# Gate and up of a transformer block: the issuing queue of the moving tiles, the places of the act sums, and the pools of the down projection

## The chip, the cores and the metric

One core of one Trainium2 chip runs the whole program. The metric is the device time of one execution in microseconds (us). The kernel before took 3004.6 us (median of three runs, 3001.72 to 3014.55).

## The reference: what is computed

The reference is one transformer block on two sequences of 1024 positions and 1024 features, in float32:

```
h = layernorm(x) * (1 + ca) + sa
x = x + ga * attention(h)
h = layernorm(x) * (1 + cb) + sb
gate = einsum(h, Wg) * ag
up   = einsum(h, Wu) * au
x = x + gb * (einsum(silu(gate) * up, Wd) * ad)
```

The attention has 32 heads of 32, a causal mask with linear position biases, and layer norms on queries and keys. Wg and Wu have 2752 rows of 1024, and Wd 1024 rows of 2752. The shifts, scales and gates (sa, ca, ga and so on) come from a product of a small vector with a modulation matrix.

## The kernel before

**Order of the work.** The program runs the modulation and the QKV projections, then the attention with dense work in between, the output projection and what is left of the rows, then gate and up (from about 1560 us to 2497 us), then down (to the end). The change lies in the last two.

**Tiling.** Gate and up use Strassen's scheme in Winograd's form on two levels. 2560 of the 2752 inner columns are cut into five slices of 512 (the index s); the other 192 are handled apart. For each slice, the outer level has seven stages (STAGES, in the order A11, A12, S1, S2, S4, S3, A22) and the inner level has seven products in each stage (CHAIN). A product is a gate matmul pair and an up matmul pair, each of four matmuls of 128x512 in the trace, on the same moving tile. The four PSUM banks of a stage are gx, ux, gy and uy: inner products that end in column x or y of the result. One product is 3.43 us of TensorE, one stage 24.0, one slice 168.2.

**Moving tiles.** `moving` (line 1648) allocates a tile bt of 512 KB in a pool of six buffers and loads it from DRAM, where the operands of both levels have been written earlier (bop_T and bop_B). The first six go through ScalarE's queue, all others through SyncE's (SP). A load waits until the product that used the buffer six loads ago has been done.

**Reads of PSUM.** `merge` (line 1566) takes each inner product out of its bank: a copy on ScalarE where there is nothing to add (1576, 1584), else an addition on VectorE (1578, 1582, 1586) into the outer results X, C, Z and T. The results of gate have one buffer each; uX has two. Within a stage several products go on accumulating in one bank, and the next matmuls into it wait for the read between; the stages take two sets of four banks in turn.

**GpSimd.** `gate_sums` (1623 to 1630) builds the outer sums of the weights of a slice, eight operations; `gate_inner` (1632) builds the inner sums (sig and siu) of each stage, eight operations in two buffers. In the first twenty stages a slice of down's weights is prepared as well: `down_load` loads wdr (1179), `down_weights` does four subtractions on GpSimd (1185 to 1188) and stores the results (wdop, 1190), with one buffer of wdr.

**Due times.** `after(n, go)` puts an operation into a list that is due when n more products have been issued; `run_due` issues those that are due after each product, and ties each to stand behind the last read of PSUM on VectorE (`behind`). So the operations beside the products are placed by product counts, while the order in each engine is what these counts give.

**Results of a slice.** `final(x_, m, q, n)` takes an outer result to its end: two Silus on ScalarE (1703) at count n, two products gate x up on VectorE (1707) at count n + 1, and a store. The act sums S1 to S4 that down's own outer level needs (two halves l, four sums each, 1783) are due 3 to 6 products after the end of the slice; SP stores each (1784). The next slice's first write into gX has to wait for the products that read the old gX.

**Down.** `stage_weights` (1837) loads the quarters B11, B12, B21, B22 of the prepared down weights for an outer stage and builds T1 to T4 on VectorE (1846 and following); act tiles (aq) are loaded at 1856, their inner sums (dsi) are built at 1862 to 1865, and the matmuls are at 1876. The pools of this part lie over space that gate and up give back.

Of the kernel before, what the change touches and what calls it, by code (L numbers as in the profile page):

```python
# [12 lines left out]
FP = mybir.dt.float32  # L13
# [5 lines left out]
P = 128  # L19
# [461 lines left out]
def kernel(  # L481
# [19 lines left out]
    nc = tc.nc  # L501
# [6 lines left out]
    HALF = D // 2  # L508
# [1079 lines left out]
    with ExitStack() as ff:  # L1588
# [9 lines left out]
        with ExitStack() as gu:  # L1598
# [45 lines left out]
                    )  # L1644
                return ins

            def moving(s, n_, i, eng=nc.sync):
                qb_ = CHAIN[i][2]
                bt = bsp.tile([P, NJ, 2, P], FP, tag="bt", name=f"bt_{s}_{n_}_{i}")
                eng.dma_start(bt, bop_dram[STAGES[n_][1]][:, INNER.index(qb_)])  # L1650
                return bt


            W = gate_weights(0, nc.scalar)
            ins = gate_inner(W, 0, 0)
            bts = [moving(0, 0, i, nc.scalar) for i in range(6)]
            rest_st.close()
            ffp.append(ff.enter_context(tc.tile_pool(name="ff_a", bufs=4, space=PSUM)))
            ptp, rxp, rcp = open_("fpart"), open_("resx"), open_("resc")
# [22 lines left out]
            for s in range(NSB):  # L1682
                if s:
                    W = gate_weights(s)
                gate_sums(W)
                res = {}

                def result(mat, x_):
                    if (mat, x_) not in res:
                        res[mat, x_] = (rxp if x_ == "X" else rcp if x_ == "C" else rzp).tile(  # L1690
                            [P, 2, 2, 512], FP, tag=f"{mat}{x_}", name=f"{mat}{x_}_{s}",
                            bufs=2 if (mat, x_) == ("u", "X") else None,
                        )
                    return res[mat, x_]

                def final(x_, m, q, n, res=res, s=s):


                    g, u = res["g", x_], res["u", x_]

                    def silu(l):
                        ib = 4 * s + 2 * m + l
                        nc.scalar.activation(g[:, l], g[:, l], AF.Silu, scale=vt[:, R_AG + ib : R_AG + ib + 1])

                    def product(l):
                        ib = 4 * s + 2 * m + l
                        r = nc.vector.scalar_tensor_tensor(
                            u[:, l], u[:, l], vt[:, R_AU + ib : R_AU + ib + 1], g[:, l], ALU.mult, ALU.mult
                        )
                        if l and q != "A21":  # L1710
                            nc.sync.dma_start(act_dram[q][:, s], u)
                        return r

                    for l in range(2):
                        after(n, lambda l=l: silu(l))
                    for l in range(2):
                        after(n + 1, lambda l=l: product(l))

                for n_, (oa, ob, frm, to) in enumerate(STAGES):
                    if (s, n_) == (0, 2):  # L1720
                        pair_st.close()
                        rzp, asp = open_("resz"), open_("asum")
                    if (s, n_) != (0, 0):
                        ins = gate_inner(W, s, n_)
                        bts = []
                    bank = {
                        (mat, c_): ffbank(f"{mat}{c_}_{s}_{n_}")
                        for mat in ("g", "u")
                        for c_ in ("x", "y")
                    }  # L1730
                    part = {"g": {}, "u": {}}
                    tiles = {
                        mat: (None if frm is None else result(mat, frm), result(mat, to)) for mat in ("g", "u")
                    }
                    i = next(slices, None)
                    if i is not None:
                        wd_ = down_load(i, dwp)
                        after(5, lambda i=i, wd_=wd_: down_weights(i, wd_))
                    for e, (c_, qa, qb_, q) in enumerate(CHAIN):
                        bt = bts[e] if e < len(bts) else moving(s, n_, e)  # L1740
                        for mat in ("g", "u"):
                            ps = bank[mat, c_]
                            for c2 in range(2):
                                nc.tensor.matmul(  # L1744
                                    ps.rearrange("p (j t) -> p j t", j=NJ), ins[mat][qa][:, c2, :], bt[:, :, c2, :],
                                    start=(q in ("P1", "P2", "P5") and c2 == 0), stop=(c2 == 1),
                                    skip_group_check=True,
                                )
                            f_, t_ = tiles[mat]
                            merge(  # L1750
                                q, ps, lambda m, n: t_[:, m, n, :],
                                None if f_ is None else (lambda m, n: f_[:, m, n, :]),
                                part[mat], ptp, f"{mat}_{s}_{n_}",
                            )
                        count[0] += 1
                        run_due()
                    if oa == "A12":
                        final("C", 0, "A11", 1)
                    elif oa == "S2":
                        for m, n in QUADS:  # L1760
                            for mat in ("g", "u"):
                                nc.gpsimd.tensor_add(
                                    result(mat, "T")[:, m, n], res[mat, "X"][:, m, n], res[mat, "Z"][:, m, n]
                                )
                    elif oa == "S3":
                        for m, n in QUADS:
                            for mat in ("g", "u"):
                                z = res[mat, "Z"][:, m, n]
                                nc.gpsimd.tensor_add(z, res[mat, "X"][:, m, n], z)
                        final("Z", 1, "A22", 5)  # L1770
                    elif oa == "S4":
                        final("T", 0, "A21", 1)
                    elif oa == "A22":
                        final("X", 1, "A12", 1)

                a11, a12, a21, a22 = (res["u", x_] for x_ in ("C", "X", "T", "Z"))
                for l in range(2):
                    sm_ = {
                        q: asp.tile([P, 2, 512], FP, tag=q, name=f"as{q}_{s}_{l}") for q in ("S1", "S2", "S4")
                    }  # L1780

                    def go(q, op, dst, x_, y_, s=s, l=l):
                        r = op(dst, x_, y_)
                        nc.sync.dma_start(act_dram[q][:, s, l], dst)
                        return r

                    for e, (q, op, dst, x_, y_) in enumerate((
                        ("S1", nc.vector.tensor_add, sm_["S1"], a21[:, l], a22[:, l]),
                        ("S2", nc.vector.tensor_sub, sm_["S2"], sm_["S1"], a11[:, l]),
                        ("S3", nc.vector.tensor_sub, a21[:, l], a11[:, l], a21[:, l]),  # L1790
                        ("S4", nc.vector.tensor_sub, sm_["S4"], a12[:, l], sm_["S2"]),
                    )):
                        after(3 + (4 * l + e) // 2, lambda go=go, r=(q, op, dst, x_, y_): go(*r))
            run_due(True)


        with tc.tile_pool(name="wdq", bufs=1) as wdp, tc.tile_pool(name="aq", bufs=3) as aqp, tc.tile_pool(
            name="wdt", bufs=1
        ) as wtp, tc.tile_pool(
            name="ais", bufs=3  # L1800
        ) as aip, tc.tile_pool(name="dres", bufs=1) as drp, tc.tile_pool(
            name="dpart", bufs=2
        ) as dpp, tc.tile_pool(name="fin", bufs=3) as fnp, tc.tile_pool(
            name="drest", bufs=1
        ) as dlp:
            gb = []
            ra = [dlp.tile([P, B, NJ, 2, P], FP, name=f"ra{r}") for r in range(2)]
            rw = [dlp.tile([P, D], FP, name=f"rw{r}") for r in range(2)]
# [25 lines left out]
                    nc.gpsimd.tensor_add(x1, x1, c_[:, th])  # L1834
                    nc.sync.dma_start(out[b, ts(2 * i + th, P), ts(n, HALF)], x1)

            def stage_weights(ob, eng):
                wt = {
                    q: (wtp if q[0] == "T" or q == "B12" else wdp).tile(
                        [P, NSB, 256], FP, tag=q, name=f"wd_{ob}_{q}", bufs=2 if q == "B22" else 1  # L1840
                    )
                    for q in ("B11", "B12", "B21", "B22", "T1", "T2", "T3", "T4")
                }
# [8 lines left out]
            def products(n_, i, wt):  # L1852
# [15 lines left out]
                    c_: ffbank(f"d{c_}_{n_}_{i}")[:, 0:256] for c_ in ("x", "y")  # L1868
                }
                if (to, i) not in res:  # L1870
                    res[to, i] = drp.tile([P, 2, HALF], FP, tag=f"{'T' if to == 'C' else to}{i}", name=f"d{to}_{i}")
                f_, t_ = None if frm is None else res[frm, i], res[to, i]
                part = {}
                for c_, qa, qb_, q in CHAIN:
# [37 lines left out]

            running = []
            for n_ in range(len(STAGES)):
                wt = stage_weights(STAGES[n_][1], nc.sync if n_ else nc.scalar)
                for i in range(NJ):
                    if n_ == 0 and i == 2:
                        rest_loads()
# [59 lines left out]
```

## Time and profile before

| Quantity | Value |
|---|---|
| Median of three runs | 3004.6 us (3001.72 to 3014.55) |
| Profiled execution, its own time | 3009.32 us |
| Span of its profile | 3007.6 us |
| Granted TensorE clock, mean | 0.962 |
| TensorE (PE) busy | 2743.3 us, 91% |
| VectorE (DVE) busy | 1506.9 us, 50% |
| GpSimd (POOL) busy | 1289.1 us, 43% |
| ScalarE (ACT) busy | 686.6 us, 23% |
| Transfers | 579.12 MB, mean 193 GB/s |

The profile is of one execution, 4.7 us above the median of the runs. "Busy" is the time in which an engine has an instruction under way; an idle engine that others don't wait for costs nothing. Lines of a timeline give the start (us from the span's start), the duration, the engine, the line of the kernel, the operation, the tiles written and read, how many instructions are joined (x), and in brackets the idle time before it and what ended it. SPq and ACTq are the queues of SyncE and ScalarE in which transfers are issued. Lines of a view of waits give the engine and line that waited, what it waited for, and the total, the number and the longest of these waits in us.

By stretches, the profile shows for gate and up:

| Stretch, us | TensorE busy | ScalarE busy | GpSimd busy | Share of DMA |
|---|---|---|---|---|
| 1603 to 1705 | 101.10 of 102 | 9.31 | 59.54 | 0.81 |
| 1705 to 1780 | 64.78 of 75 | 8.09 | 43.36 | 0.79 |
| 1780 to 1843 | 41.06 of 63 | 4.06 | 41.08 | 0.72 |
| 1843 to 1963 | 120.00 of 120 | 11.01 | 57.87 | 0.66 |
| 1963 to 2497 | 515.12 of 534 | 55.37 | 261.13 | 0.65 |

The first slice and the first part of the second lie before 1843, the slices 2, 3 and 4 after 1963.

### The profile page before, as it was taken

The page shows a single profiled execution, that of the slowest core. Times are in us where ns is not written, and L with a number is a line of the kernel's source. Part 1 is how long each engine was busy: PE and PEld are TensorE (multiplying, and loading weights), DVE is VectorE, ACT ScalarE, POOL GpSimd, SP SyncE. Part 2 cuts the span into 40 slices and gives each one's busy share as a digit, 9 for nine tenths or more (in the row PEclk, how much of TensorE's full clock was granted, in tenths as well). Part 3 has the DMA queues.
Part 4 walks back from the last instruction along what each step waited for, and adds up shares of the span by engine and source line. Part 5 has one row for each costly group of instructions (what it writes and reads, how often), then busy time and mean ns, then how long its engine had stood idle before and what let it go on. Part 6 is the DMA issues. An engine that isn't in the chain of part 4 may idle for free.

```text
span 3007.6 us, 29795 instructions
## 1 busy us (share of the span) xinstructions
PE 2743.3 (91%) x10271; PEld 1341.0 (45%) x10271; DVE 1506.9 (50%) x2285; ACT 686.6 (23%) x1523; POOL 1289.1 (43%) x1150
## 2 busy tenths in 40 slices
PE   7999999999998879787996978999999998999998
PEld 2444333333332222223662433434444346888776
DVE  5666424566443456555553334464634545444453
ACT  1322144444434455552110011010101100000000
POOL 3211033334354555654465564564735441222343
PEclk9999999999999899998997999999999998999999
DMA  9877753534525545335777777675666659554542
GB/s 338 295 257 292 265 210 113 188 130 157 190 88 194 140 150 165 103 109 151 219 244 245 242 248 255 183 260 166 223 218 193 218 164 274 147 158 139 150 143 78
DMA packets 377571, 579.12 MB, mean 193 GB/s; under 512 B 21590, under 2 KB 278712, under 8 KB 366276
## 3 DMA queue, kind: packets, MB, share of 16 engines
q1 hardware_dynamic: 359768, 554.54, 56.5%
q10 hardware_dynamic: 17644, 22.59, 2.5%
q8 instruction: 84, 1.38, 0.2%
q14 instruction: 75, 0.61, 0.1%
HBM read 411.89 MB, written 165.17 MB: 192 GB/s over the span
## 4 chain that ended last, share of the span: by engine, by line
PE 39%; DMA 7%; POOL 6%; issue 5%; DVE 3%; ACT 1%; SPq 1%; POOLq 0%; ACTq 0%; DVEq 0%
PE gx L1744 7%; PE ux L1744 6%; PE dx L1876 6%; PE dy L1876 5%; PE gy L1744 5%; PE uy L1744 4%; PE bank L745 2%; PE sc L745 1%; DMA wdr<-in_L_ffn_Wd_dram 1%; ACT p L1053 1%; DMA wdop_T<-wdr 1%; PE rest L745 1%; DMA bt<-bop_B 1%; PE av L745 1%; POOL p L1085 1%
## 5 line engine op out<-in xcount | busy, mean ns | idle before, releaser
L1053 ACT ACTIVATE p<-sc,kw 128x128 f32<-128x128 f32 (+3 forms) x1024 | 422.1, 514 | 335.2 <-PE sc L745 324.0
L745 PE MATMUL bank<-wT,a 128*128 128x512 f32 x768 | 361.9, 614 | 14.1 <-DVE wT L814 7.2
L1085 POOL TENSOR_TENSOR p<-p,p 128x1024 f32<-128x1024 f32 (+3 forms) x128 | 264.2, 2064 | 252.3 <-PE av L745 223.4
L1085 DVE TENSOR_TENSOR p<-p,p 128x1024 f32<-128x1024 f32 (+3 forms) x192 | 247.5, 1301 | 119.4 <-POOL p L1057 70.5
L745 PE MATMUL bank<-wB,a 128*128 128x512 f32 x576 | 263.8, 602 | 2.1 <-DVE raw L947 1.3
L745 PE MATMUL sc<-cq,ck 32*128 32x512 f32 (+3 forms) x1536 | 195.0, 549 | 68.8 <-ACT p L1053 68.6
L1057 POOL TENSOR_SCALAR_AFFINE_SELECT p<-p 128x256 f32<-128x256 f32 x256 | 137.5, 548 | 229.5 <-ACT p L1053 226.3
L745 PEld LDWEIGHTS bank<-wT,a 128*128 128x128 f32 x768 | 142.5, 195 | 201.2 <-issue 181.0
L745 PE MATMUL av<-p,cv 128*32 128x512 f32 (+3 forms) x1536 | 170.6, 512 | 4.7 <-POOL p L1057 4.7
L745 PEld LDWEIGHTS bank<-wB,a 128*128 128x128 f32 x576 | 104.4, 190 | 146.9 <-issue 127.6
L1744 PE MATMUL gy<-bt,sig 128*128 128x512 f32 x280 | 139.4, 622 | 27.4 <-DVE gX L1582 13.2
L745 PEld LDWEIGHTS sc<-cq,ck 32*128 32x128 f32 x1536 | 65.6, 188 | 199.8 <-ACT p L1053 118.1
L1744 PE MATMUL gx<-bt,sig 128*128 128x512 f32 x280 | 134.9, 605 | 4.4 <-DMA bt<-bop_T 2.3
L1744 PE MATMUL uy<-bt,siu 128*128 128x512 f32 x280 | 132.2, 594 | 0.6 <-DMA bt<-bop_B 0.6
L1744 PE MATMUL ux<-bt,siu 128*128 128x512 f32 x280 | 131.6, 592 | 0.0
L949 DVE TENSOR_TENSOR raw<-P,bank 128x512 f32<-128x512 f32 x48 | 32.9, 685 | 158.0 <-PE bank L745 142.7
L1744 PEld LDWEIGHTS gy<-bt,sig 128*128 128x128 f32 x280 | 54.6, 198 | 98.7 <-issue 80.4
L1744 PEld LDWEIGHTS gx<-bt,sig 128*128 128x128 f32 x280 | 54.2, 196 | 76.9 <-issue 74.6
L745 PEld LDWEIGHTS av<-p,cv 128*32 128x32 f32 x1536 | 33.4, 110 | 121.3 <-issue 87.6
L1744 PE MATMUL gx<-bt,wgA 128*128 128x512 f32 x120 | 58.4, 610 | 28.5 <-DVE gX L1582 27.9
L1744 PEld LDWEIGHTS uy<-bt,siu 128*128 128x128 f32 x280 | 53.5, 191 | 68.7 <-issue 68.0
L1744 PEld LDWEIGHTS ux<-bt,siu 128*128 128x128 f32 x280 | 53.2, 190 | 67.0 <-issue 66.3
(416 smaller groups left out, 4583.5 us busy)
## 6 DMA issues: line engine op xcount, KB each, us to landing
bt<-bop_T SPq DMA_DIRECT2D x140, 512.0 KB
bt<-bop_B SPq DMA_DIRECT2D x99, 512.0 KB
a<-hop SPq DMA_DIRECT2D x20, 1792.0 KB
wm<-in_L_wmod_dram SPq DMA_DIRECT2D x48, 512.0 KB
wB<-in_L_attn_Wqkv_dram SPq DMA_DIRECT2D x21, 1024.0 KB
aq_S<-act_S SPq DMA_DIRECT2D x16, 1280.0 KB
qk<-qs SPq DMA_DIRECT2D x16, 1024.0 KB
act_S<-asS SPq DMA_DIRECT2D x30, 512.0 KB
```

The costliest lines, as they stand in the source:

```text
L745: return in_order(nc.tensor.matmul(*args, **kw_))
L949: nc.vector.tensor_add(dst, part_t[MATE[q]], bank)
L1053: nc.scalar.activation(p[:, g, lo:hi], sp[:, g, lo:hi], AF.Exp, bias=kw[:, d, h_ : h_ + 1])
L1057: nc.gpsimd.affine_select(out=p[:, :, 0:P], in_=p[:, :, 0:P], pattern=[[0, 2], [1, P]], compare_op=ALU.is_ge, fill=0.0, base=0, channel_mu ...
L1085: adders[b](half, jb).tensor_add(dst, dst, ps[half][:, :, 0:n])
L1744: nc.tensor.matmul(ps.rearrange("p (j t) -> p j t", j=NJ), ins[mat][qa][:, c2, :], bt[:, :, c2, :], start=(q in ("P1", "P2", "P5") and c2 ...
L1876: nc.tensor.matmul(bank[c_], ins[qa][:, s, :], wt[qb_][:, s, :], start=(q in ("P1", "P2", "P5") and s == 0), stop=(s == NSB - 1), skip_gro ...
```

## The change

1. All moving tiles are issued from ScalarE's queue.
2. In `final`, the second product gate x up is due one count after the first instead of together with it.
3. The act sums are put into the list at the end of stage S3 and not at the end of the slice. Z's Silus are due at count z = 4 (2 in the last slice) instead of 5. S1, S2 and S3 of the two halves are due at z + 2 to z + 4, which is around the end of the slice, and S4 at 11 and 12, counted from the end of S3. S2 has two buffers.
4. The pools of down are opened in another order and packed otherwise: the second buffer of B22 becomes a pool of its own for odd stages (`late`), the X results have a pool of their own, and the inner sums of act have two buffers instead of three. Which of the tiles lie over space that is free early changes with this.

```diff
-            def moving(s, n_, i, eng=nc.sync):
+            def moving(s, n_, i):
                 qb_ = CHAIN[i][2]
                 bt = bsp.tile([P, NJ, 2, P], FP, tag="bt", name=f"bt_{s}_{n_}_{i}")
-                eng.dma_start(bt, bop_dram[STAGES[n_][1]][:, INNER.index(qb_)])
+                nc.scalar.dma_start(bt, bop_dram[STAGES[n_][1]][:, INNER.index(qb_)])
                 return bt
...
                     for l in range(2):
-                        after(n + 1, lambda l=l: product(l))
+                        after(n + 1 + l, lambda l=l: product(l))
+
+                def act_sums(z, res=res, s=s):
+                    a11, a12, a21, a22 = (res["u", x_] for x_ in ("C", "X", "T", "Z"))
+
+                    def go(q, op, dst, x_, y_, l):
+                        r = op(dst, x_, y_)
+                        nc.sync.dma_start(act_dram[q][:, s, l], dst)
+                        return r
+
+                    for l in range(2):
+                        s1, s2, s4 = (
+                            asp.tile([P, 2, 512], FP, tag=q, name=f"as{q}_{s}_{l}", bufs=2 if q == "S2" else 1)
+                            for q in ("S1", "S2", "S4")
+                        )
+                        for e, r in enumerate((
+                            ("S1", nc.vector.tensor_add, s1, a21[:, l], a22[:, l]),
+                            ("S2", nc.vector.tensor_sub, s2, s1, a11[:, l]),
+                            ("S3", nc.vector.tensor_sub, a21[:, l], a11[:, l], a21[:, l]),
+                            ("S4", nc.vector.tensor_sub, s4, a12[:, l], s2),
+                        )):
+                            n = 7 + 4 + l if e == 3 else z + 2 + (3 * l + e) // 2
+                            after(n, lambda r=r, l=l: go(*r, l))
...
-                        final("Z", 1, "A22", 5)
+
+                        z = 4 if s < NSB - 1 else 2
+                        final("Z", 1, "A22", z)
+                        act_sums(z)
...
-                        after(3 + (4 * l + e) // 2, lambda go=go, r=(q, op, dst, x_, y_): go(*r))
...
+        with ExitStack() as dn:
+            wdp, aqp, wtp, aip, dpp, dxp, late, drp, fnp, dlp = (
+                dn.enter_context(tc.tile_pool(name=n, bufs=k))
+                for n, k in (
+                    ("wdq", 1), ("aq", 3), ("wdt", 1), ("ais", 2), ("dpart", 2), ("dresx", 1),
+                    ("wdl", 1), ("dres", 1), ("fin", 3), ("drest", 1),
+                )
+            )
...
-            def stage_weights(ob, eng):
+            def stage_weights(ob, odd, eng):
                 wt = {
-                    q: (wtp if q[0] == "T" or q == "B12" else wdp).tile(
-                        [P, NSB, 256], FP, tag=q, name=f"wd_{ob}_{q}", bufs=2 if q == "B22" else 1
+                    q: (wtp if q[0] == "T" or q == "B12" else late if q == "B22" and odd else wdp).tile(
+                        [P, NSB, 256], FP, tag=q, name=f"wd_{ob}_{q}"
                     )
...
-                wt = stage_weights(STAGES[n_][1], nc.sync if n_ else nc.scalar)
+                wt = stage_weights(STAGES[n_][1], n_ % 2, nc.sync if n_ else nc.scalar)
```

More of the change, by code (lines that the diff above doesn't have):

```diff
@@ L1655 @@
             ins = gate_inner(W, 0, 0)
-            bts = [moving(0, 0, i, nc.scalar) for i in range(6)]
+            bts = [moving(0, 0, i) for i in range(6)]
             rest_st.close()
@@ L1774 @@
                         final("X", 1, "A12", 1)
[L1776 to L1792, printed above, removed]
-                        after(3 + (4 * l + e) // 2, lambda go=go, r=(q, op, dst, x_, y_): go(*r))
-            run_due(True)
[L1797 to L1805, printed above, removed]
+            run_due(True)
+        with ExitStack() as dn:
[6 more added lines that the diff above has]
+            )
             gb = []
@@ L1870, in products @@
                 if (to, i) not in res:
-                    res[to, i] = drp.tile([P, 2, HALF], FP, tag=f"{'T' if to == 'C' else to}{i}", name=f"d{to}_{i}")
+                    res[to, i] = (dxp if to == "X" else drp).tile([P, 2, HALF], FP, tag=f"{'T' if to == 'C' else to}{i}", name=f"d{to}_{i}")
                 f_, t_ = None if frm is None else res[frm, i], res[to, i]
```

## Prediction

> **What bounds the kernel now.** I first read the page: TensorE is busy 91% of the span and the granted clock is 0.96, so only idle TensorE can be won. The change touches nothing before the gate/up part, so I then asked the waits of TensorE from 1590 us (end of the rest rows) to 2530 us (first products of down); columns are total us, times, longest:
>
> ```profile
> PE gx L1744 <- DVE gX L1582: 27.9, 1, 27.9
> PE gy L1744 <- DMA bt<-bop_B: 26.4, 6, 11.5
> PE gy L1744 <- DVE gX L1582: 13.2, 3, 4.5
> PE dx L1876 <- DVE dsi_A L1863: 11.6, 1, 11.6
> PE gx L1744 <- DMA bt<-bop_T: 4.9, 5, 1.8
> ...
> PE dx L1876 <- DMA aq_A<-act_A: 2.6, 1, 2.6
> ```
>
> Four places hold nearly all of it: one wait at the start (27.9, ended 1603.9), the moving tiles (26.4 + 4.9 and smaller ones, some 37 in all, mostly before 1825), three boundaries between slices (13.2), and the start of down (11.6 + 2.6).
>
> *Moving tiles.* The timeline of SP's queue where the two longest waits lie (the ones that end at 1796.65 and 1819.86):
>
> ```profile
> 1792.97 1.34 SPq L1784 DMA_DIRECT2D act_S<-asS  x2
> 1795.34 0.32 SPq L1784 DMA_DIRECT2D act_S<-uT  x1
> 1796.58 13.60 SPq L1784 DMA_DIRECT2D act_S<-asS  x3
> 1813.14 0.32 SPq L1784 DMA_DIRECT2D act_S<-uT  x1
> 1814.80 0.32 SPq L1784 DMA_DIRECT2D act_S<-asS  x1
> 1815.21 3.36 SPq L1650 DMA_DIRECT2D bt<-bop_B  x6
> ```
>
> No moving tile is issued for 22 us, because stores of the act sums wait for VectorE in the same queue. Six come out at once when they are through.
>
> *A boundary.* TensorE, VectorE and GpSimd where slice 2 begins (1963.32):
>
> ```profile
> 1973.62 1.88 PE L1744 MATMUL uy<-bt,siu 128*128 128x512 f32 x4
> 1979.93 3.78 PE L1744 MATMUL gy<-bt,sig 128*128 128x512 f32 x4 [4.43 <-DVE gX L1582]
> 1983.50 2.91 PE L1744 MATMUL gx<-bt,sig 128*128 128x512 f32 x4
> ```
> ```profile
> 1971.05 4.95 DVE L1707 SCALAR_TENSOR_TENSOR uX<-uX,vt,gX 128x1024 f32<-128x1024 f32 x2
> 1975.92 3.35 DVE L1783 TENSOR_TENSOR asS<-uT,uZ 128x1024 f32<-128x1024 f32 x1
> 1979.20 0.67 DVE L1582 TENSOR_TENSOR gX<-g_P,gy 128x512 f32<-128x512 f32 x1
> ```
> ```profile
> 1974.88 3.32 POOL L1630 TENSOR_TENSOR wgS<-wgA,wgS 128x1024 f32<-128x1024 f32 x1
> ```
>
> A read of PSUM (0.67) stands behind two products and a sum, which alternate with GpSimd's gate sums. A boundary costs 4.43 of waiting, 2.9 of slower matmuls after it (3.78 + 2.91 against 1.88 twice), and 1.6 for moving tiles a little later. Slices 2, 3 and 4 take 177.95 each against 7 x 7 x 3.433 = 168.2 of matmuls: 9.75 lost each.
>
> *Start of down.* 2512.60 + 2.32 is followed by an idle 11.65:
>
> ```profile
> 2526.56 3.75 PE L1876 MATMUL dx<-wd_B_T,dsi_A 128*128 128x256 f32 x8 [11.65 <-DVE dsi_A L1863]
> ```
> ```profile
> 2497.38 1.27 ACTq L1845 DMA_DIRECT2D wd_B_B<-in_L_ffn_Wd_dram  x1
> ```
> ```profile
> 2513.28 1.49 DVE L1846 TENSOR_TENSOR wd_B_T<-wd_B_B,wd_B_B 128x1280 f32<-128x1280 f32 x1 [4.55 <-DMA wd_B_B<-in_L_ffn_Wd_dram]
> ```
>
> The first down weight that lies over gate/up's moving tiles is issued only when TensorE has done with them (2497.18) and takes 15.9 us to land; weight sums, act sums and input sums then follow on VectorE.
>
> **What the Trainium skill says.** "DMA: Bandwidth & Descriptors", section Issuing engines are not separate DMA queues: transfers begun by ScalarE and SyncE run on the same 16 DMA engines, and another issuer saves only issuing time. The trace adds to it: issue is 0.42 us for a moving tile, but SP's queue is in order, and what is to be won is its 22 us of standing behind a store's wait, not bandwidth. "SBUF — State Buffer", section SBUF: two separate sides: VectorE with two SBUF inputs and GpSimd exclude each other for a whole instruction. The trace agrees: a 128x1024 sum on VectorE takes 1.22 alone (2504.01) and 3.35 beside gate sums, which go from 2.35 to 3.33. "TensorE: Matmul & The Clock Gate", section What's actually happening: after an idle window of about 3.4 us the clock halves until as long a busy time is over. That alone would cost 1.7; the trace shows 2.9 after 4.43 us idle, and I use that.
>
> **The change, part by part.**
>
> 1. *239 moving tiles to ScalarE's queue.* Added: 239 x 0.42 = 100 us of issuing on ScalarE, which is busy 55 of the 534 us of slices 2 to 4. A tile's wait is for the product six before it; behind it in ScalarE's queue stand copies out of PSUM and Silus of later products, so its wait ends before they are due. Bounds 0 to +10 (an issue of 0.4 delaying one copy per boundary and stage); I take 0. Removed: in slices 0 and 1 the waits for tiles. What is late next? SP's down-weight chain (load wdr, four subtractions on GpSimd, store wdop, one buffer) now runs without tiles between, and in the changed program's order GpSimd has all slices up to the nineteenth before the inner sums of slice 1's second stage (before: up to the sixteenth). From the starts of L1185 the chain's period is 9.0 to 15 us, mean 11.6, while it shared SP; periods without a tile's wait in between are 9 to 11, and I take 10.3. The changed order has one more slice done by 1626. So the nineteenth is done at 1626 + 15 x 10.3 = 1780; inner sums of 8 (as 1958.41 to 1966.16), gate sums of 24 (1966.86 to 1991.35) and 5 for the first inner sums on them give 1817 for the start of slice 1's third stage. Before it starts at 1843: **gain 26**; TensorE alone would be there at about 1803, so at most 40. At a period of 9.1 the bound is 40, at 11 it is 15; each 1 us more costs 15.
> 2. *The wait of 27.9* (1603.9): VectorE stands behind inner-product buffers whose stores (bop, landing 6.28 us after 1596.45) queue on SP among tiles. Without four tile issues there: **gain 3**, bounds 0 to 6.
> 3. *Silu's second product one count later and act sums earlier.* Nothing is removed. In VectorE's new order the reads between two big operations are single, but ahead of the read that frees gy's bank for the next slice's third product now stand S1, S2, S3 of both halves, both products and S4 of the first: six more sums than the one of before. From 1962.5 (second product of Z done): S1 1.7, read 0.7, S2 1.7 (beside inner sums) to 1966.6; then read 0.7, S3, S1 3.3 each, read 0.7, S2, S3 3.3 each, products 4.9, S4 3.3, read 0.7 end at 1990.1, 27 after the slice's start, where it was 16.6. gy was due 12.2 after the start, and TensorE's new order puts 2.6 us more of other matmuls ahead of it: the wait is 27 - 14.8 = 12.2, with the ramp 2.9 15.1, against 4.43 + 2.9 + 1.6 = 8.9. To these 6 I add 1 for reads that then stand behind S4 of the second half. **Loss 7 at each of three, 21 in all.** Bounds: -1.6 each if the sums run without GpSimd (tile waits gone, nothing else worse), +12 if each of the eleven big operations takes 3.35 and S1's store delays the second S1. The boundary 0 to 1 is held by GpSimd anyway (step 1): nothing.
> 4. *Act sums of the last slice from count 2, down's tiles over free space.* Three sums are done before gate/up ends; after E = 2497.18 stand the second half's three sums (1.22 each), two products (1.28), S4 (1.22), then T1 1.49, dsi 0.81, T2 1.48, dsi 0.81: 7.4 + 4.6, about E + 12 to 13, since B11, B21 and B22 no longer wait for TensorE's end. The first six products of down cover 13. Before: waits 2.64 + 11.65 and slower matmuls after them (4.11 and 3.75 for 2.32 and 1.87), 18 in all; I leave 6 of it (a wait of 3 and a ramp of 2.9). **Gain 12**; bounds 5 (3.9 for three sums, as at 2514.69, when GpSimd collides) and 17 (nothing left). ais 3 to 2 buffers and B22's two places: covered by the products of a whole stage; 0, bounds 0 to +5.
>
> **Sum** against the profiled execution (3007.6 span, 3009.3 run): -26 - 3 + 21 - 12 = -20, 2989. That execution is 4.7 above the median of 3004.6; the same 20 off the median gives **2985**. A change within 0.5% (15 us) can't be told from none.
>
> **Rivals.**
> - *Boundaries don't get worse* (sums hide beside GpSimd, or finish early): 21 comes back, 2964. For it: VectorE idles 5.18 just before 1970.44. Against: eight gate sums occupy GpSimd right through this stretch.
> - *Nothing to see*: period 11 (gain 15) and boundaries of +10 each: -15 - 3 + 30 - 12 = 0, 3004. For it: the mean period is nearer to this than to 10.3.
> - *Slower*: the down-weight chain becomes the bound. With tiles at full rate (DMA share already 0.81 from 1603 to 1705) loads and stores of wdr take longer; from a period of 11.6 the whole gain is gone, at 13 slice 1's third stage starts 40 later, 1857, and the sum is +14 - 3 + 21 - 12 = +20: 3025. For it: three of the first five periods are 12 to 15. Against: those had a tile's wait on SP in them.
> - That tiles don't leave SP is excluded by the new order of the queues.
>
> **Chances.** Forecast 0.40 (own range 2970 to 2993, a little of it within 0.5%), boundaries as before 0.13, nothing 0.27, slower 0.20. Faster by over 0.5%: 0.50; within: 0.30; slower: 0.20. The range from 2958 to 3018 takes in the first three and the bounds of steps 1 and 3, and leaves most of the slower case out.
>
> **What would show it.** Step 1: no wait on bop_B over 2 us; waits of gx, gy on GpSimd's sig or wgS around 1750 to 1820; L1185 starts 10 apart; slice 1's third stage near 1817. Step 3: in slices 2 to 4 a wait for gX L1582 of 10 to 15 in place of 4.4, slices of 184. Step 4: no wait over 6 for dsi_A after the last gate/up product. Slices of 178 or less, or a chain period over 11.6, make the prediction wrong.

## The result and the profile after

The changed kernel takes 3024.6 us (median of 12 runs, 3018.5 to 3035.0), the kernel before 3010.8 beside it (12 runs, 3001.7 to 3016.2; the three shown before the prediction gave 3004.6): a ratio of 1.0053, 95% interval 1.0039 to 1.0068. It is slower by half a per cent. The forecast was 2985, 0.8% faster.

The profiled execution of the changed kernel has a span of 3020.8 us against 3007.6, a difference of 13.2. The matmuls of gate and up are in the same order in both but for ten in the first stage of each of slices 1 to 4, so the span can be cut at the same three products. "Stage 0.1" is the second stage of the first slice. What the matmuls alone need is 192.3 us in the second stretch and 504.7 in the third.

| Stretch, us | Before | After | Difference |
|---|---|---|---|
| start to stage 0.1 | 1610.5 | 1603.6 | -6.9 |
| stage 0.1 to 1.2 (slices 0 and 1) | 232.7 | 268.0 | +35.4 |
| stage 1.2 to 4.2 (three boundaries) | 533.9 | 536.3 | +2.4 |
| stage 4.2 to the end (start of down in it) | 630.6 | 612.9 | -17.7 |

So all of the loss lies in slices 0 and 1, where the tiles were to bring a gain. The waits of TensorE of the changed kernel from 1590 to 2560 us:

```profile
PE gx L1769 <- DMA bt<-bop_T: 20.7, 7, 12.6
PE gy L1769 <- DVE gX L1582: 15.1, 4, 5.5
PE uy L1769 <- DVE uX L1582: 12.5, 4, 3.1
PE gx L1769 <- POOL wdr L1185: 10.7, 1, 10.7
PE gx L1769 <- ACT g_U L1576: 6.4, 1, 6.4
...
PE gy L1769 <- DMA bt<-bop_B: 0.4, 1, 0.4
```

Tiles from bop_B, the largest item before (26.4), are gone. Tiles from bop_T have taken their place (4.9 before, 20.7 now), and two waits are new: for inner sums that stand behind a slice of down's weights on GpSimd (10.7), and for a copy on ScalarE (6.4). The first of the two, on GpSimd and TensorE:

```profile
1638.43 0.72 POOL L1641 TENSOR_TENSOR sig<-wgS,sig 128x256 f32<-128x256 f32 x1
1644.00 0.72 POOL L1185 TENSOR_TENSOR wdr<-wdr 128x256 f32<-128x256 f32 x1 [4.85 <-DMA wdr<-in_L_ffn_Wd_dram]
1644.68 0.72 POOL L1638 TENSOR_TENSOR siu<-wuS 128x256 f32<-128x256 f32 x1
```
```profile
1645.37 3.75 PE L1769 MATMUL gx<-bt,sig 128*128 128x512 f32 x4 [10.72 <-POOL wdr L1185]
```

GpSimd is idle for 4.85 us with the inner sums siu ready to be made, because a slice of down's weights is ahead of them in its order and its load has not landed. The copy stands in ScalarE's queue behind the issue of a tile that is itself held (the second of the two):

```profile
1653.38 6.92 ACTq L1650 DMA_DIRECT2D bt<-bop_T  x2
1660.40 0.58 ACT L1576 COPY g_U<-gx 128x512 f32<-128x512 f32 x1 [14.64 <-DMA wdr<-in_L_ffn_Wd_dram]
```

The tiles are late although ScalarE's queue has little else to do. ScalarE's queue, SP's queue and GpSimd, side by side:

```profile
1733.21 0.33 ACTq L1650 DMA_DIRECT2D bt<-bop_T  x1
1738.51 0.33 ACTq L1650 DMA_DIRECT2D bt<-bop_T  x1
1743.04 0.33 ACTq L1650 DMA_DIRECT2D bt<-bop_T  x1
```
```profile
1734.04 2.11 SPq L1179 DMA_DIRECT2D wdr<-in_L_ffn_Wd_dram  x4
...
1743.81 1.91 SPq L1179 DMA_DIRECT2D wdr<-in_L_ffn_Wd_dram  x4
```
```profile
1728.91 0.72 POOL L1185 TENSOR_TENSOR wdr<-wdr 128x256 f32<-128x256 f32 x1 [4.29 <-DMA wdr<-in_L_ffn_Wd_dram]
...
1738.57 0.73 POOL L1185 TENSOR_TENSOR wdr<-wdr 128x256 f32<-128x256 f32 x1 [6.52 <-DMA wdr<-in_L_ffn_Wd_dram]
```

A tile goes out at 1738.51, when the loads of a slice of down's weights have landed (its first subtraction starts at 1738.57). The next goes out at 1743.04, when that slice's stores have landed (the next load starts at 1743.81). So two tiles leave in each period of that chain, from 1690 to 1779 one every 5.2 us, where TensorE wants one every 3.43. Their buffers had been free for 20 to 26 us (the last matmuls of the products six before start at 1708.21, 1712.32 and 1723.11). Bandwidth is not what is short: from 1605 to 1840 the changed kernel moves 230 GB/s, the kernel before 250.

The listing of the program's queues tells how this can be. Each transfer has one of eight counters of landings, whichever of the two queues issues it, and its issue waits until the transfer before it on the same counter has landed, as well as for TensorE. The trace shows which landings these are: of the 32 tiles issued from 1619 to 1779, 30 go out 0.02 to 0.15 us after a landing on their own counter, and on 29 of these the transfer before was a load or store of the chain. The prediction took such waits to be SP's alone.

The longest tile wait has another cause. Its tile goes out 8.7 us after the last landing on its counter, right behind a Silu of gZ in ScalarE's queue. The Silu needs a sum gZ of GpSimd, and that stands behind slices of down's weights. GpSimd, ScalarE and TensorE:

```profile
1791.65 1.26 POOL L1794 TENSOR_TENSOR gZ<-gX,gZ 128x512 f32<-128x512 f32 x1
```
```profile
1792.95 1.15 ACT L1703 ACTIVATE gZ<-gZ,vt 128x1024 f32<-128x1024 f32 x1 [44.27 <-DMA wdr<-in_L_ffn_Wd_dram]
1793.03 0.33 ACTq L1650 DMA_DIRECT2D bt<-bop_T  x1
```
```profile
1799.05 3.75 PE L1769 MATMUL gx<-bt,sig 128*128 128x512 f32 x4 [12.60 <-DMA bt<-bop_T]
```

The bracket of the Silu names a landing, but the sum on GpSimd ends at 1792.91, just before it.

### The profile page after: what moved, and what is told of

The parts are those of the page before. It is cut to its first block, busy times and chain, and to the rows that moved or that the text cites. A ratio compares the mean times of both kernels' runs of the same rounds, so it can differ in the third digit from the quotient of the medians.

```text
span 3020.8 us, 29771 instructions
## 1 busy us (share of the span) xinstructions
PE 2747.5 (91%) x10271; PEld 1342.6 (44%) x10271; DVE 1466.0 (49%) x2285; ACT 685.1 (23%) x1523; POOL 1270.3 (42%) x1150
## 4 chain that ended last, share of the span: by engine, by line
PE 38%; DMA 8%; POOL 6%; issue 4%; DVE 4%; ACT 1%; SPq 1%; POOLq 0%; ACTq 0%; DVEq 0%
PE dx L1884 6%; PE ux L1769 6%; PE gx L1769 6%; PE gy L1769 5%; PE dy L1884 5%; PE uy L1769 4%; DMA wdr<-in_L_ffn_Wd_dram 2%; PE bank L745 2%; DMA wdop_T<-wdr 1%; PE sc L745 1%; ACT p L1053 1%; DVE asS L1725 1%; PE rest L745 1%; DMA aq_A<-act_A 1%; PE av L745 1%
## 5 line engine op out<-in xcount | busy, mean ns | idle before, releaser
L1769 PE MATMUL gx<-bt,sig 128*128 128x512 f32 x280 | 143.4, 637 | 60.0 <-ACT g_U L1576 29.3
L745 PE MATMUL rest<-hl,restw 128*128 128x256 f32 x288 | 69.1, 400 | 14.7 <-DMA restw<-in_L_ffn_Wu_dram 14.7
```

The source lines that it names most:

```text
L745: return in_order(nc.tensor.matmul(*args, **kw_))
L1769: nc.tensor.matmul(ps.rearrange("p (j t) -> p j t", j=NJ), ins[mat][qa][:, c2, :], bt[:, :, c2, :], start=(q in ("P1", "P2", "P5") and c2 ...
```

## Experiments

All parts were put on the kernel before alone or taken from the changed one. The interval of each ratio is against the kernel before on the same chip (3006.8, 3008.4, 3010.5 and 3010.9 us in four groups). The last three columns are of one profiled execution each, up to 7 us from the median of its kernel (that of "pools, paced" is 7.0 above).

| Kernel | Median, us | Ratio, 95% | Stage 0.1 to 1.2 | 1.2 to 4.2 | 4.2 to end |
|---|---|---|---|---|---|
| before | 3010.8 | 1 | 232.7 | 533.9 | 630.6 |
| changed | 3024.6 | 1.0053, 1.0039 to 1.0068 | 268.0 | 536.3 | 612.9 |
| tiles only | 3026.0 | 1.0056, 1.0039 to 1.0072 | 261.6 | 522.9 | 625.4 |
| changed, no tiles | 3009.0 | 1.0006, 0.9995 to 1.0017 | 229.5 | 552.9 | 614.3 |
| pools only | 2989.1 | 0.9932, 0.991 to 0.9953 | 230.1 | 532.6 | 615.4 |
| changed, fewer DMAs | 3052.8 | 1.0148, 1.0126 to 1.0169 | 285.6 | 532.6 | 611.5 |
| changed, chain on GpSimd | 3089.8 | 1.0272, 1.0244 to 1.0301 | 309.6 | 539.0 | 612.0 |
| tiles, old order | 2991.1 | 0.9937, 0.9917 to 0.9957 | 232.7 | 524.0 | 626.6 |
| changed, old order | 3003.5 | 0.9971, 0.996 to 0.9982 | 238.5 | 543.3 | 617.6 |
| changed, paced | 2972.0 | 0.9869, 0.985 to 0.9888 | 213.2 | 548.2 | 612.7 |
| pools, paced | 2965.5 | 0.9848, 0.9829 to 0.9867 | 208.8 | 541.8 | 616.3 |
| tiles and pools, paced | 2938.8 | 0.9767, 0.9739 to 0.9795 | 200.5 | 527.5 | 613.6 |

The theories at the start: A, the chain of down's weights sets the pace of tiles and inner sums; B, Silus of Z, due one count earlier, wait for GpSimd in ScalarE's queue and hold the tiles behind them; C, the DMA engines are saturated.

### The parts alone

Tiles alone (the kernel before, `eng=nc.scalar` as the default):

```diff
-            def moving(s, n_, i, eng=nc.sync):
+            def moving(s, n_, i, eng=nc.scalar):
```

> The kernel before with the moving tiles on ScalarE's queue, nothing else. Theory A (a tile's issue waits for landings of the down-weight chain in any queue, and the new order puts three more slices of down weights ahead of slice 1's second stage): 20 to 32 us slower than before, the loss between 1600 and 1875 us, boundaries and the start of down as before. Theory B (Silus of Z, due one count earlier, wait for GpSimd in ScalarE's queue and hold the tiles): at most 10 us slower, since the Silus stand where they stood. Theory C (the 16 DMA engines are saturated by tiles at full rate): 20 to 32 us slower, as A.

It costs 17 to 19 us, just under what A and C gave and more than the whole change loses, in the same stretch (+28.9), while its boundaries gain 11. B falls as a cause of the loss: the Silus are due where they were, and the loss is there. But a Silu of gZ holds the longest tile wait here too (11.93 us, 12.60 in the changed kernel), because GpSimd makes its sum late. In this part B and A meet.

The changed kernel with the tiles on SP again (`eng=nc.sync` as the default in `moving`, the first six on ScalarE):

> The changed kernel with the moving tiles back on SP's queue; act sums, products and pools as changed. Theories A and C: the loss of 28 before slice 2 goes and the gain of 17 at the start of down stays: 10 to 20 us faster than before. Theory B: the same, since the Silus then hold no tiles. If the act sums' new places cause the loss: as slow as the changed kernel.

It is as fast as the kernel before, not 10 to 20 faster, and 15.7 faster than the changed kernel: the loss of slices 0 and 1 and the gain at the end came as expected, but the boundaries cost 19.1 more in its place. VectorE and TensorE of this kernel where slice 2 begins (1955.04):

```profile
1963.06 2.64 DVE L1725 TENSOR_TENSOR asS<-uT,uZ 128x1024 f32<-128x1024 f32 x1 [3.76 <-DMA act_S<-asS]
...
1972.19 6.63 DVE L1707 SCALAR_TENSOR_TENSOR uX<-uX,vt,gX 128x1024 f32<-128x1024 f32 x2
1978.74 3.35 DVE L1725 TENSOR_TENSOR asS<-uX,asS 128x1024 f32<-128x1024 f32 x1
1982.02 0.68 DVE L1582 TENSOR_TENSOR gX<-g_P,gy 128x512 f32<-128x512 f32 x1
```
```profile
1982.75 3.78 PE L1769 MATMUL gy<-bt,sig 128*128 128x512 f32 x4 [11.85 <-DVE gX L1582]
```

The read that frees gy ends 27.7 us after the start of the slice; the prediction had 27. The second half's first sum waits 3.76 us for the store of the first half's from the one buffer of S1, which the prediction had only as a bound; that the totals agree is in part luck.

Down's pools alone (the pools and `stage_weights` of the change on the kernel before):

> The kernel before with down's pools as changed, nothing else. If the 17 us at the start of down come from the weights landing early: 10 to 15 us faster than before, with no wait over 6 us on dsi_A. If they come from the act sums being early: within 5 us of before, and a wait of 8 or more on dsi_A remains.

It is 18 to 20 us faster, more than expected, but not for the reason in the expectation: the wait on dsi_A is still there.

```profile
2517.92 4.04 PE L1875 MATMUL dx<-wd_B_T,dsi_A 128*128 128x256 f32 x10 [11.32 <-DVE dsi_A L1862]
```

Its cause is no longer the late weight but the act sums ahead of dsi_A on VectorE, two of them 3.90 long. What is gone are the wait for aq_A with its slow matmuls (2.64 + 1.8) and four waits for d_P at later stages of down (6.8 in all, with slow matmuls after them). These four waits are in all three profiles with the old pools and in none of the eleven with the new ones. So the pools give 15.2 of the 17.7 at the end. With the early act sums as well the stretch takes 614.3, and with the tiles 612.9: some 1 us each, no more than such profiles can tell.

### How the chain holds the tiles

Fewer transfers in the chain: two loads and one store for a slice, into one tensor, instead of four and four (the changed kernel otherwise):

```diff
-        for kh in range(2):
-            for n in range(2):
-                nc.sync.dma_start(w[:, 2 * kh + n], rows_[:, 2 * kh : 2 * kh + 2, ds(n * HALF + c_ * P, P)])
+        for n in range(2):
+            nc.sync.dma_start(w[:, 4 * n : 4 * n + 4], rows_[:, :, ds(n * HALF + c_ * P, P)])
...
-        for o, r in (("T1", 0), ("T2", 4), ("T3", 1), ("T4", 2)):
-            nc.sync.dma_start(wd_dram[o][:, s, :, ts(c_, P)], w[:, r])
+        nc.sync.dma_start(wd_all[:, :, s, :, ts(c_, P)], w.rearrange("p (o l) c -> p o l c", o=4))
```

> The changed kernel with a slice of down's weights moved by 2 loads and 1 store instead of 4 and 4, the same bytes, subtractions and buffer. Theory A (transfers in flight are what is short: tiles wait for landings of the chain's many small ones): 20 to 35 us faster than the changed kernel, tile waits under 5 us in all, chain period 8 to 10. Theory C (bandwidth): within 6 us of the changed kernel, since the bytes are the same. Theory B: within 10 us of it, with the longest tile wait still behind a Silu of gZ.

All missed: it is 28 us slower than the changed kernel. The chain's period is not shorter (12.8 us between subtractions from the fifth slice to the last, against 11.85), and the tiles still go out with its landings, in twos and threes. The number of transfers is not what holds them. The stretch is longer by another 17.5, as much as stage 1.0 is (53.4 us, 36.0 in the changed kernel). There VectorE's second sum S1 waits for a store of the first from the one buffer, which SP issues at 1841.0, behind the chain's last store (1837.05):

```profile
1849.35 2.16 DVE L1722 TENSOR_TENSOR asS<-uT,uZ 128x1024 f32<-128x1024 f32 x1 [18.57 <-DMA act_S<-asS]
```

The rest of the 28 lies before stage 0.1.

The chain's loads and stores issued by GpSimd (`nc.gpsimd.dma_start` in `down_load` and `down_weights` of the changed kernel); in the listing, its landings then have counters of their own:

> The changed kernel with the loads and stores of the down-weight chain issued by GpSimd instead of SP; their bytes, order and dependences are unchanged. In the order of the queues the tiles' issues then wait for no landing of the chain any more. Theory A in its narrow form (a tile's issue is held by landings of the chain): tile waits under 5 us in slices 0 and 1, chain period about as before, 15 to 30 us faster than the changed kernel. If tiles are late for want of bandwidth or for Silus ahead of them in ScalarE's queue: tile waits of 15 or more stay, within 8 us of the changed kernel or slower, for GpSimd's issuing.

The tiles behave as A says: in stages 0.3 to 0.6 nearly all go out 0.6 to 1.1 us after their product of six before has begun its last matmul. One tile wait of 11.3 is left, and its tile again stands behind a Silu of gZ (1860.08). ScalarE's queue and TensorE:

```profile
1657.70 0.33 ACTq L1650 DMA_DIRECT2D bt<-bop_T  x1
...
1661.29 0.33 ACTq L1650 DMA_DIRECT2D bt<-bop_T  x1
```
```profile
1655.78 1.88 PE L1769 MATMUL uy<-bt,wuS 128*128 128x512 f32 x4
...
1694.11 3.41 PE L1769 MATMUL gx<-bt,sig 128*128 128x512 f32 x4 [12.41 <-POOL sig L1639]
```
```profile
1756.70 0.69 DVE L1578 TENSOR_TENSOR g_P<-gT,gx 128x512 f32<-128x512 f32 x1 [38.96 <-POOL gT L1787]
```

But the kernel is slower still, for now everything that GpSimd makes comes late: it issues eight transfers of 0.72 us a slice itself, and the chain's period is 16.4. TensorE waits 17.4 us for inner sums, and 33.6, 14.4 and 13.3 for VectorE's reads that need the sums gT and gZ of GpSimd. So the chain holds TensorE in more than one way: by landings through the tiles and the copies behind them, and on GpSimd through the inner sums and the sums gT and gZ. Freeing one leaves the others. The expected gain did not come.

### The order of the slices

The listing of GpSimd's queue has slices 0 to 16 of down's weights ahead of the inner sums of stage 1.1 in the kernel before, and all of them, 0 to 19, in the changed kernel and in the one with the tiles alone (the expectation counts from 0 too). The planner that lays out each engine's order does this; that it does so because SP is emptier is argued, not shown. A tie puts the first subtraction of each slice behind the inner sums of a given stage, on the same engine and with no wait added; at[i] is the stage that slice i follows in the kernel before:

```diff
+        first = nc.gpsimd.tensor_sub(w[:, 0], w[:, 1], w[:, 0])
+        if i:
+            behind(first, inner_last[at[i]])
```

Put on the kernel with the tiles alone:

> The kernel before with the tiles on ScalarE's queue, and the slices of down's weights tied on GpSimd to the places that they have in the kernel before (16 of them ahead of slice 1's second stage, not 19). If the loss of 17 to 19 us of the tiles alone comes from the slices run further ahead: it goes, and the three boundaries' gain of 3.4 each stays, 2990 to 3003. If it comes from ScalarE's queue itself (tiles held by landings, copies and Silus held by tiles): still 10 to 20 us slower than before, 3018 to 3028.

The loss is gone, 28.9 us in the stretch from 0.1 to 1.2, with the tiles still on ScalarE's queue: 0.63% faster than before. And that stretch takes 232.7, as in the kernel before: tiles off SP are worth nothing there in sum. The waits are not the same: those for tiles fall from 31 to 10, and waits for inner sums (12.9) and a copy (6.1) take their place. The gain is at the boundaries (9.9) and after.

On the whole changed kernel:

> The changed kernel, whole, with the slices of down's weights tied on GpSimd to the places that they have in the kernel before. If the order of these slices is all that turned the forecast over: tiles alone with the old order (2991) less the pools' 20 plus the 10 to 20 of the act sums, 2980 to 2996, faster than before by about what the prediction said. If the act sums add to the loss in slices 0 and 1 as well: 3000 or more.

It is 0.29% faster than before, 29.5 better in that stretch than the changed kernel, and worse at the boundaries (38.6 beyond the matmuls, changed 31.6, tiles with the old order 19.3). So the second case of the expectation came. The order explains the sign, but not all: the act sums cost some 20 at the three boundaries and 6 in the stretch before. The reverse, the new order with the tiles on SP, was not run.

One slice a stage instead (the tie behind the inner sums of the slice's own stage), on the changed kernel, on the pools alone, and on tiles and pools:

> The changed kernel with the subtractions of each slice of down's weights tied on GpSimd behind the inner sums of its own stage: one slice a stage, instead of up to three ahead of a stage's inner sums. Theory A (the chain of down weights, run ahead of its stage, sets the pace of tiles and inner sums in slices 0 and 1): the 66 us lost there in the changed kernel (268 for eight stages of 24 and one boundary) go but for the boundary: 2955 to 2975. If the loss comes from the queue of the tiles alone (ScalarE blocked by copies and Silus): within 10 us of the changed kernel.

> The kernel before with down's pools as changed, and the same tie; tiles on SP. Theory A: the tile waits of 35 us in slices 0 and 1 shrink to those behind the act sums' stores at the boundary (10 to 20): 2960 to 2975, against 2989 without the tie. If SP's order alone makes those waits: 2980 to 2990.

> The kernel before with tiles on ScalarE's queue, down's pools as changed and the tie; act sums and products where they were before. Theory A, with what the parts alone showed (boundaries 6.0 with tiles on ScalarE, 9.3 with the act sums moved too): 2943 to 2960, faster than both the paced ones beside it. If moving tiles off SP is worth nothing once the chain is paced: as slow as the paced kernel with tiles on SP.

All three came within or just below what was expected. The last is the fastest, 2.3% under the kernel before. Its waits from 1590 to 2530 us:

```profile
PE gy L1747 <- DVE gX L1585: 12.8, 4, 4.6
PE dx L1878 <- DVE dsi_A L1865: 9.3, 1, 9.3
PE gx L1747 <- POOL sig L1642: 3.8, 1, 3.8
PE gx L1747 <- POOL sig L1643: 3.4, 1, 3.4
```

No tile is waited for. It moves 260 GB/s from 1605 to 1840, against 230 in the changed kernel, so C falls too. Once paced, tiles on ScalarE gain 27 (2938.8 against 2965.5), and act sums early lose 33 (2972.0 against 2938.8). With the tiles on SP the paced kernel has these waits at its four boundaries, and with the tiles on ScalarE they are gone:

```profile
PE gy L1747 <- DMA bt<-bop_B: 19.2, 4, 7.6
```

That is the gain which the prediction saw, in tiles that stand behind stores of the act sums; it comes only when the chain is out of the way.

Two variants of this fastest kernel: the act sums early in the last slice alone (with z = 2 there), and the products one count apart with the act sums late (`after(n + 1 + l, ...)`).

> The fastest so far (tiles on ScalarE, down's pools as changed, down weights one slice a stage; 2939) with the act sums moved early in the last slice alone, where no next slice waits behind them. If the wait on dsi_A at the start of down (9.3 there) is theirs: it falls under 4 and the kernel is 2 to 8 us faster than that one, 2931 to 2937. If other waits take its place (act tiles, weights): within 2 us of it.

2938.5 us, ratio 0.9768 (0.975 to 0.9785): no gain. The wait on dsi_A is gone, and waits for aq_A (5.3) and dX (1.0) stand in its place.

> The same fastest kernel with only the products of gate and up one count apart, act sums late as in the kernel before. If the 33 us that act sums and products cost together (2972 against 2939) come from the act sums standing ahead of the reads at a slice's start: within 4 us of 2939. If the spacing of the products costs a part: 2945 to 2960.

2936.6 us, ratio 0.9769 (0.9745 to 0.9794): the spacing of the products costs nothing, so the 33 us are those of the act sums, with Z's Silus one count earlier.

## Why the prediction was wrong

**Tiles, forecast -26, measured +35.4 in slices 0 and 1.** This is the step that failed, in two statements. The first: "A tile's wait is for the product six before it; ... so its wait ends before they are due", with a cost of 0. On ScalarE's queue the tiles wait for landings of the down-weight chain, and their pace is the chain's: two tiles a period. A copy behind such a tile comes 6.4 us late, and a Silu ahead of another holds it for the longest wait (12.6); the prediction looked only at what stands behind a tile, and took it for ready. With the old order the stretch takes 232.7 with tiles on either queue, so nothing was to be won there by leaving SP.

The second is the path: last slice, inner sums, gate sums, then stage 1.2. Its period, taken as 10.3, is 11.85 (L1185 from 1620.4 to 1798.2, 15 periods), so the nineteenth slice was done at 1801, not 1780. Put into the prediction's own sum, that gives 1838 for stage 1.2 instead of 1817. This takes most of the gain away, and makes no loss. The other 33 us to the measured 1871.6 come on a path that the prediction did not have: the slices run ahead delay inner sums and tiles of every stage on the way, so that TensorE reaches stage 1.0 only at 1811.6. Stage 1.1 then runs without a wait (24.0), and gate sums don't hold stage 1.2 at all. The prediction saw the new order and priced only its last slice, as a date for one inner sum. With the tiles on ScalarE the order costs 29 (tiles alone and changed kernel, each with and without it).

The 0.42 us for a tile's issue, which made 100 us of issuing, holds for slices 0 and 1; the median of all 239 on SP is 0.32, and on ScalarE 0.33. It decided nothing.

**Start, forecast -3, measured -6.9.** The wait that was 27.9 ends earlier, but 4.5 of the 6.9 were there before gate and up began; other kernels scatter by as much, and no more is claimed.

**Act sums, forecast +21 at three boundaries, measured +2.4 in the changed kernel.** The mechanism and the size fit where tiles stay on SP: +19.1 (from 29.2 beyond the matmuls to 48.2). But the forecast was for tiles on ScalarE, and there two things are different. Tiles on ScalarE alone make the boundaries 11.0 better (18.2; the prediction had 1.6 each). From that 18.2 the changed kernel is at 31.6, so the act sums cost 13.4. VectorE, GpSimd and TensorE of the changed kernel where slice 2 begins (1991.79):

```profile
2009.08 2.47 DVE L1707 SCALAR_TENSOR_TENSOR uX<-uX,vt,gX 128x1024 f32<-128x1024 f32 x2
...
2014.76 0.67 DVE L1582 TENSOR_TENSOR gX<-g_P,gy 128x512 f32<-128x512 f32 x1
```
```profile
2010.32 3.43 POOL L1627 TENSOR_TENSOR wuS<-wuS,wuA 128x1024 f32<-128x1024 f32 x1 [3.38 <-DMA wuA<-in_L_ffn_Wu_dram]
```
```profile
2015.49 1.98 PE L1769 MATMUL gy<-bt,sig 128*128 128x512 f32 x4 [2.48 <-DVE gX L1582]
```

GpSimd waits 3.38 us for the load of wuA, and meanwhile both products run without its sums beside them, in 2.47 us (forecast 4.9; 6.63 with tiles on SP). The read that frees gy ends 23.6 us after the start of the slice, not 27, and TensorE waits 3.13 (for uX) and 2.48, not 12.2. The prediction also put the boundary from slice 0 to 1 at nothing: paced, stage 1.0 lasts 43.6 with early act sums and 27.6 with late ones.

**Start of down, forecast -12, measured -17.7.** Right in sign, wrong in its parts. Early weights alone did not end the wait on dsi_A (11.32 is left with the new pools); with early act sums as well it is gone. Early act sums with the old pools were not run. Most of the gain came from what the prediction had at "0" or as a part: the pools' packing ends four waits for d_P and the wait for aq_A.

**The rivals.** The slower one named the place (the down-weight chain), the period from which the gain is gone (11.6; it is 11.85) and 3025 us. It had 0.20, for the chain was thought to slow down for want of DMA bandwidth. It did not need that: more of it was put ahead. By the prediction's own sum 6 of the 26 are still there at 11.6, and the gain is gone at 12. That 3025 is nearly the measured 3024.6 is luck: its parts were +14, -3, +21 and -12 from 3004.6, and the measured ones are +35.4, -6.9, +2.4 and -17.7. The range to 3018 left it out by its own choice. "Boundaries don't get worse" was nearly right in the number, by two effects that cancel.

The Trainium skill's "DMA: Bandwidth & Descriptors", section Issuing engines are not separate DMA queues, was cited for saying that another issuer saves only issuing time. Slices 0 and 1 agree where the order is kept: 232.7 us with the tiles on either queue. The paced kernels differ from it: there the same move brings 27 us, for it also takes the tiles out from behind SP's waits.

## What to carry to other kernels

A transfer that is moved to another queue leaves behind the instructions ahead of it, not every wait of its own, and it gets others ahead of it and behind it: read what its issue waits for, what stands before it, and look for a rhythm (here tiles that leave with the landings of another chain). When work off the critical path is let run ahead on an engine that also feeds the critical path, count what stands behind each piece of it, at every stage and not only at the last; tying such work to the stage that it belongs to took a few lines and brought 1.7% on the changed kernel (3024.6 to 2972.0) and 0.8% on the pools alone (2989.1 to 2965.5). Of a change with several parts, try each alone: here one was worth -20, one +17 or -19 by the order of a third engine, and one +20.

## What the runs showed that had not been expected

A chain of load, four subtractions and store with 512 KB through one buffer has a period of some 12 us in both cuts that were tried: 11.85 with eight transfers a slice, 12.8 with three. Issued by GpSimd, a transfer occupies that engine for 0.72 us (four loads 2.88), and the period is 16.4; on ScalarE's queue the issue of a tile takes 0.33, and on SP's 0.32 (most of slices 2 to 4) to 0.47 (slices 0 and 1). When a tile's issue on ScalarE has to wait for the landing of a transfer of SP on the same counter, it goes out 0.02 to 0.15 us after that landing.
